# Laying the exponentials of a cross-attention block by quarters of the keys before their regrouping transfers

## The chip, the cores and the metric

The kernel runs on one core of one Trainium2 chip. The metric is the time on the device in microseconds, lower being better. The time before is a median of 3 runs.

## The reference

Two cross-attention layers follow each other, with 4 batches of 1024 queries (512 features) and 1024 context rows (384 features), all in float32. The change is in layer 0, which has 16 heads of 64:

```python
h = layernorm(x, gamma, beta)
Q, K, V = h @ Wq, context @ Wk, context @ Wv          # 16 heads of 64
attn = softmax(Q K^T, over the 1024 keys) * 64**-0.5
x = x + (attn V) @ Wo + bo
```

Layer 1 has 16 heads of 32, rotates and normalises its queries and keys, takes a softmax over the same 1024 context rows, and adds its output to x.

## The kernel before

**Tiling.** Batches follow each other. Within layer 0 of a batch the heads are taken in 8 pairs p, and within a pair the queries in 8 tiles i of 128. One step (p, i) is `Attention0.step`. Two steps of one pair make a block (`BQ = 2`), so a batch has 32 blocks and the kernel has 128.

**A step.** `scores` (L372) multiplies 128 queries by 1024 keys for both heads of the pair, into two PSUM tiles `s`. For each head VectorE takes the negative maximum of a row (L393), and ScalarE writes the exponentials to the tile `e` of the block and sums them in the same instruction (L394). VectorE then transposes `e` in place, in blocks of 32 x 32 (L399). This leaves the keys of a 32 x 32 block on the partitions, but only within each group of 32 partitions. At the end of a block, 16 transfers from SBUF to SBUF (L406) regroup the rest: transfer (g, q) takes the quarter g of the keys from the 32 partitions that held the queries of group q, and puts it on the 32 partitions of group g in the tile `eT`. VectorE inverts the sums (L410).

**Product.** `product` (L451) multiplies the values by `eT` for a whole block, as 16 matmuls in the program (8 groups of keys, 2 heads), each over 256 queries. A block is kept in `self.blocks` and its product is issued two blocks later in program order: in an even step, when two blocks are waiting. `factors` (L424) spreads the inverted sums on GpSimd, `factors_turned` (L442, L443) turns them over through TensorE and copies them to `vals` on ScalarE, and L458 multiplies them with the product.

**Buffers.** `e` and `eT` have two buffers each (tags `e` and `big`), which layer 1 also uses. The exponentials of a block so wait for the transfers of the block two before. `s` has two buffers, one for each head, so the scores of a step wait for the exponentials of the step before.

**Order.** The order on each engine is the program's. Other TensorE work (projections of later pairs at L158, output projections, layer 1's first projections) stands in a list of units, `work`, each with a cost in microseconds, and `fill` issues units between the parts of a step. All loads and stores, and the 16 transfers of a block, stand on SP's queue in program order. At the start of a pair, loads of weights (`pair_load`, L313; `wo_load`, L665), loads of x (L287) and, in the first pairs of later batches, stores of the batch before (L848) stand between two blocks' transfers. L188 and L279 load context rows and x rows. Layer 1 (L599 to L657) follows, with its own exponentials, sums (L615, L619), rotations (L501) and products (L638, L649).

Of the kernel before, what the change touches and what calls it, by code (L numbers as in the profile page):

```python
# [30 lines left out]
F32 = mybir.dt.float32  # L31
AF = mybir.ActivationFunctionType
# [3 lines left out]
P = 128  # L36
S = 1024
# [70 lines left out]
def xattn_kernel(ctx: ExitStack, tc: tile.TileContext, a: dict, out: bass.AP):  # L108
    nc = tc.nc
# [4 lines left out]
    sb = ctx.enter_context(tc.tile_pool(name="sb", bufs=2))  # L114
# [54 lines left out]
    def flush():  # L169
        while posts:  # L170
            posts.pop(0)()
# [185 lines left out]
    BQ = 2  # L357
    r = [slice(j * HD0, (j + 1) * HD0) for j in range(2)]

    class Attention0:  # L360
# [20 lines left out]
        def step(self, p, i, pr, us):  # L381
            n = f"{self.b}_{p}_{i}"
            sc = self.scores(p, i, pr)
            if i % BQ == 0 and len(self.blocks) == 2:
                self.factors_turned()
            m = sb.tile([P, 2], F32, tag="m", bufs=3, name=f"m_{n}")
            l = sb.tile([P, 2], F32, tag="l", bufs=3, name=f"l_{n}")
            if i % BQ == 0:
                self.e = sb.tile([P, BQ, 2, S], F32, tag="e", bufs=2, name=f"e0_{n}")
                self.li = sb.tile([P, BQ, 2], F32, tag="li", bufs=4, name=f"li_{n}")  # L390
            e = [self.e[:, i % BQ, j, :] for j in range(2)]
            for j in range(2):
                nc.vector.tensor_reduce(m[:, j : j + 1], sc[j], AX.X, ALU.max, negate=True)  # L393
                nc.scalar.activation(e[j], sc[j], AF.Exp, bias=m[:, j : j + 1], accum_out=l[:, j : j + 1])  # L394
            holds["posts"] = True
            self.u.fill(min(us, 1.8))
            holds["posts"] = False
            for j in range(2):
                nc.vector.transpose(e[j], e[j])  # L399
            flush()  # L400
            if i % BQ == BQ - 1:
                eT = sb.tile([P, 2 * BQ, 4, S // 4], F32, tag="big", bufs=2, name=f"eT_{n}")
                of = self.e.rearrange("p t h s -> p (t h) s")
                for g in range(4):
                    for q in range(4):
                        nc.sync.dma_start(  # L406
                            eT[32 * g : 32 * (g + 1), :, q, :],
                            of[32 * q : 32 * (q + 1), :, g * (S // 4) : (g + 1) * (S // 4)],
                        )
            nc.vector.reciprocal(self.li[:, i % BQ, :], l)  # L410
            if i % BQ == BQ - 1:
                eT = eT.rearrange("p (t h) a s -> p h t a s", h=2)
                self.blocks.append((p, i // BQ, pr, eT, self.li))
            elif self.blocks:
                if len(self.blocks) == 2:
                    self.product()
                self.factors()
            self.u.fill(us - min(us, 1.8))
# [322 lines left out]
    for b in range(B):  # L741
# [6 lines left out]
        for p in range(NPAIR):  # L748
# [15 lines left out]
            elif p % 2 == 0:  # L764
                i = p // 2 - 1
# [4 lines left out]
                    lambda n, i=i: wo[i][:, n % 2, :],  # L770
# [29 lines left out]
            for i in range(NT):  # L800
# [8 lines left out]
                n = NT * (NPAIR - p if later else 1) - i  # L809
# [15 lines left out]
        q = rotated_chains(qT, xnT, NQ, lambda k, wq=wq: wq[0][:, k, :], f"q1_{b}_0", tmp)  # L825
# [25 lines left out]
        for half in range(2):  # L851
            n = 0
# [94 lines left out]
```

## Time and profile before

| | |
|---|---|
| median of 3 runs | 2992.65 us (2991.08 to 2992.93) |
| profiled execution: time / span | 2989.95 us / 2987.7 us |
| mean granted TensorE clock | 0.996 |
| busy: TensorE / VectorE / ScalarE / GpSimd | 98% / 75% / 48% / 14% |
| packets on SP's queue | 371,664, with 343.43 MB |
| regrouping transfers L406 | 2048 of 128 KB |

A row of the costliest groups reads: line, engine, operation, output<-input by tile name, shape, count | busy us in total, mean ns of one | idle us of the engine just before them, and what ended most of it. A row of the timeline reads: start us, length us, engine, line, operation, tiles, count, and in brackets the idle time before it with what ended it; a "q" after the engine's name means its queue. A row of the windows reads: the stretch, its length, the busy time of each engine in it (TensorE, its weight loads, VectorE, ScalarE, GpSimd) with instruction counts, the granted share of the TensorE clock, the busy share of the DMA engines and GB/s.

### The profile page before, as it was taken

What the parts mean: (1) busy time and instruction counts of PE and PEld (TensorE: products, weight loads), DVE (VectorE), ACT (ScalarE), POOL (GpSimd) and SP (SyncE); (2) the same over time, 40 slices, a digit from 0 to 9 for tenths busy, and PEclk for the clock granted to TensorE, in tenths of its full rate; (3) what the DMA queues carried; (4) which work ended last, traced back from release to release, by engine and by line L of the source; (5) the groups of instructions that cost most, each with busy time, mean ns of one, the idle gap of its engine ahead of it and who ended that gap; (6) DMA issues with size and microseconds to landing.
All of it is one profiled execution on the core that took longest, in us unless ns stands there. A gap on an engine that the chain in (4) does not pass through costs nothing.

```text
span 2987.7 us, 60793 instructions
## 1 busy us (share of the span) xinstructions
PE 2917.3 (98%) x24748; PEld 1544.2 (52%) x24748; DVE 2230.7 (75%) x2824; ACT 1429.5 (48%) x2265; POOL 416.6 (14%) x392
## 2 busy tenths in 40 slices
PE   8999999999999999999999999999999999999998
PEld 5544546555544555655554454555455445455544
DVE  4777795877777779587777777958777777795777
ACT  3444443666443444465644344446664444444664
POOL 0010022420000002232000000223200000022310
PEclk9999999999999999999999999999999999999999
DMA  5788674010387867301048776730104978772000
GB/s 148 169 192 180 158 178 112 22 35 25 81 203 185 186 163 171 94 21 35 25 98 207 175 183 166 171 84 21 35 25 113 205 176 182 170 169 69 2 2 30
DMA packets 374134, 348.50 MB, mean 117 GB/s; under 512 B 37600, under 2 KB 355296, under 8 KB 373856
## 3 DMA queue, kind: packets, MB, share of 16 engines
q1 hardware_dynamic: 371664, 343.43, 48.4%
q8 instruction: 197, 3.23, 0.5%
q10 hardware_dynamic: 2192, 1.19, 0.2%
q14 instruction: 81, 0.66, 0.1%
HBM read 67.64 MB, written 8.39 MB: 25 GB/s over the span
## 4 chain that ended last, share of the span: by engine, by line
PE 78%; DVE 10%; DMA 4%; SPq 3%; ACT 2%; issue 1%; POOL 1%; DVEq 0%; ACTq 0%
PE s L372 14%; PE av L451 13%; PE po L158 10%; PE pv L158 7%; PE s L599 7%; PE av L638 6%; PE pqT L158 6%; PE pkT L158 5%; PE q_p L158 3%; DMA eT<-e 2%; SPq L406 2%; PE av L649 2%; DVE both L615 2%; DVE e L399 2%; PE k_p L158 1%; DVE m L393 1%
## 5 line engine op out<-in xcount | busy, mean ns | idle before, releaser
L394 ACT ACTIVATE e<-s,m 128x1024 f32<-128x1024 f32 x512 | 565.6, 1109 | 679.2 <-DVE m L393 613.8
L393 DVE TENSOR_REDUCE m<-s 128x1 f32<-128x1024 f32 x512 | 602.8, 1219 | 320.0 <-PE s L372 320.0
L399 DVE STREAM_TRANSPOSE e<-e 128x1024 f32<-128x1024 f32 x512 | 606.7, 1224 | 54.9 <-ACT e L394 43.0
L609 ACT ACTIVATE e<-s 128x1024 f32<-128x1024 f32 x512 | 496.5, 1022 | 315.1 <-PE s L599 300.1
L372 PE MATMUL s<-qk 64*128 64x512 f32 x2048 | 520.5, 615 | 6.0 <-ACT e L394 5.3
L451 PE MATMUL av<-eT,v 128*64 128x256 f32 x4096 | 474.8, 385 | 15.6 <-DMA eT<-e 13.7
L615 DVE TENSOR_TENSOR both<-e 128x512 f32<-128x512 f32 x512 | 342.4, 701 | 127.7 <-ACT e L609 92.5
L451 PEld LDWEIGHTS av<-eT,v 128*64 128x64 f32 x4096 | 289.4, 138 | 214.0 <-issue 53.7
L372 PEld LDWEIGHTS s<-qk 64*128 64x128 f32 x2048 | 181.8, 186 | 262.6 <-issue 188.9
L599 PE MATMUL s<-q,k 32*128 32x256 f32 x4096 | 305.7, 402 | 5.8 <-ACT q L526 2.7
L599 PEld LDWEIGHTS s<-q,k 32*128 32x128 f32 x4096 | 191.6, 185 | 149.7 <-ACT e L609 71.4
L158 PE MATMUL po<-wo,vals 128*128 128x512 f32 x512 | 239.6, 601 | 2.5 <-ACT v L130 2.5
L158 PE MATMUL pqT<-hT,w 128*128 128x512 f32 (+1 forms) x800 | 241.3, 597 | 0.7 <-ACT hT L255 0.7
L443 ACT COPY vals<-rT 128x256 f32<-128x256 f32 x128 | 47.7, 372 | 327.4 <-PE rT L442 327.4
L301 DVE TENSOR_TENSOR x<-x,po 128x512 f32<-128x512 f32 x200 | 133.8, 679 | 82.8 <-PE po L158 82.8
L158 PEld LDWEIGHTS pv<-w,cT 128*128 128x128 f32 (+1 forms) x2400 | 176.7, 152 | 30.3 <-issue 27.2
L158 PE MATMUL pv<-w,cT 128*128 128x128 f32 (+1 forms) x2400 | 186.5, 275 | 0.0
L158 PE MATMUL pkT<-cT,w 128*128 128x512 f32 (+1 forms) x600 | 181.6, 599 | 1.1 <-ACT cT L130 1.1
L619 DVE TENSOR_TENSOR both<-both 128x1024 f32<-128x1024 f32 x128 | 159.7, 1248 | 4.4
L158 PEld LDWEIGHTS po<-wo,vals 128*128 128x128 f32 x512 | 90.9, 190 | 106.4 <-issue 101.4
L158 PEld LDWEIGHTS pqT<-hT,w 128*128 128x128 f32 (+1 forms) x800 | 85.9, 151 | 112.2 <-issue 105.9
L638 PE MATMUL av<-e,v 128*32 128x256 f32 x2048 | 137.0, 385 | 0.0
(461 smaller groups left out, 2667.0 us busy)
## 6 DMA issues: line engine op xcount, KB each, us to landing
eT<-e SPq DMA_DIRECT2D x2048, 128.0 KB, 2.8
xr<-in_x_dram SPq DMA_DIRECT2D x32, 256.0 KB, 4.3
x<-in_x_dram SPq DMA_DIRECT2D x32, 256.0 KB, 3.8
wo<-in_Wo_dram SPq DMA_DIRECT2D x16, 512.0 KB, 4.2
out_dram<-x SPq DMA_DIRECT2D x32, 256.0 KB, 2.7
w<-in_Wq_dram SPq DMA_DIRECT2D x31, 256.0 KB, 4.0
c<-in_ctx_dram SPq DMA_DIRECT2D x32, 192.0 KB, 4.5
wkv<-in_wkv_dram SPq DMA_DIRECT2D x16, 384.0 KB, 3.5
```

The source lines that it names most:

```text
L158: nc.tensor.matmul(o[rr], lhsT[:, rr], rhs, start=start, stop=stop)
L301: nc.vector.tensor_add(xt[t], xt[t], pp[0])
L372: nc.tensor.matmul(sc[j][:, kb * 512 : (kb + 1) * 512], pr["qT"][r[j], i * P : (i + 1) * P], pr["kT"][r[j], kb * 512 : (kb + 1) * 512], st ...
L393: nc.vector.tensor_reduce(m[:, j : j + 1], sc[j], AX.X, ALU.max, negate=True)
L394: nc.scalar.activation(e[j], sc[j], AF.Exp, bias=m[:, j : j + 1], accum_out=l[:, j : j + 1])
L399: nc.vector.transpose(e[j], e[j])
L451: nc.tensor.matmul(av[r[j], :W].rearrange("p (t a i) -> p t a i", t=BQ, a=4), pr["v"][:, k, r[j]], eT[:, j, :, :, k * 32 : (k + 1) * 32], ...
L599: nc.tensor.matmul(sc[j // 2][:, j % 2, c, :], kT[rr, g, k * P : (k + 1) * P], qT[rr, g, qb * WQ : (qb + 1) * WQ], start=True, stop=True,)
L609: nc.scalar.activation(e, sc[u], AF.Exp, scale=float(np.sqrt(np.float32(HD1))))
L615: nc.vector.tensor_add(self.both[:, kk, 2 * u : 2 * u + 2, :], es[u][:, :, 0, :], es[u][:, :, 1, :])
L619: nc.vector.tensor_add(self.both[:, 0], self.both[:, 0], self.both[:, kk])
L638: nc.tensor.matmul(self.av[rr, 0, :], v[g][:, 2 * kk + c, rr], es[j // 2][:, j % 2, c, :], start=first and c == 0, stop=end and c == 1,)
```

## The change

The tile `e` was laid by step, head and key. It is now laid by quarter of the keys first, and then by step and head. The exponentials of one step and head are written as four pieces of 256, a quarter apart, and the transposes read and write the same four pieces. The tile `eT` is laid by group of queries first, and then by step and head. So a regrouping transfer moves, for each of its 32 partitions, one piece of 4 KB on both sides, where it moved four pieces of 1 KB. Bytes, the number of transfers, their order and the arithmetic are the same. The product reads the same elements of `eT` at other distances.

```diff
             if i % BQ == 0:
-                self.e = sb.tile([P, BQ, 2, S], F32, tag="e", bufs=2, name=f"e0_{n}")
+                self.e = sb.tile([P, 4, BQ * 2, S // 4], F32, tag="e", bufs=2, name=f"e0_{n}")
                 self.li = sb.tile([P, BQ, 2], F32, tag="li", bufs=4, name=f"li_{n}")
-            e = [self.e[:, i % BQ, j, :] for j in range(2)]
+            e = [self.e[:, :, i % BQ * 2 + j, :] for j in range(2)]
             for j in range(2):
                 nc.vector.tensor_reduce(m[:, j : j + 1], sc[j], AX.X, ALU.max, negate=True)
-                nc.scalar.activation(e[j], sc[j], AF.Exp, bias=m[:, j : j + 1], accum_out=l[:, j : j + 1])
+                nc.scalar.activation(e[j], sc[j].rearrange("p (g s) -> p g s", g=4), AF.Exp, bias=m[:, j : j + 1], accum_out=l[:, j : j + 1])
...
             if i % BQ == BQ - 1:
-                eT = sb.tile([P, 2 * BQ, 4, S // 4], F32, tag="big", bufs=2, name=f"eT_{n}")
-                of = self.e.rearrange("p t h s -> p (t h) s")
+                eT = sb.tile([P, 4, BQ * 2, S // 4], F32, tag="big", bufs=2, name=f"eT_{n}")
                 for g in range(4):
                     for q in range(4):
-                        nc.sync.dma_start(
-                            eT[32 * g : 32 * (g + 1), :, q, :],
-                            of[32 * q : 32 * (q + 1), :, g * (S // 4) : (g + 1) * (S // 4)],
-                        )
+                        nc.sync.dma_start(eT[32 * g : 32 * (g + 1), q], self.e[32 * q : 32 * (q + 1), g])
             nc.vector.reciprocal(self.li[:, i % BQ, :], l)
             if i % BQ == BQ - 1:
-                eT = eT.rearrange("p (t h) a s -> p h t a s", h=2)
+                eT = eT.rearrange("p a (t h) s -> p h t a s", h=2)
                 self.blocks.append((p, i // BQ, pr, eT, self.li))
```

## The prediction

> **What bounds the kernel now.** I read the busy table first, then the costliest groups, then the list of waits of TensorE, then the timeline at the longest of those waits.
>
> ```profile
> PE 2917.3 (98%) x24748; PEld 1544.2 (52%) x24748; DVE 2230.7 (75%) x2824; ACT 1429.5 (48%) x2265; POOL 416.6 (14%) x392
> ...
> L399 DVE STREAM_TRANSPOSE e<-e 128x1024 f32<-128x1024 f32 x512 | 606.7, 1224 | 54.9 <-ACT e L394 43.0
> ...
> L451 PE MATMUL av<-eT,v 128*64 128x256 f32 x4096 | 474.8, 385 | 15.6 <-DMA eT<-e 13.7
> ```
>
> TensorE is busy 98% of the span: 2987.7 - 2917.3 = 70.4 us is all that is open. What the change touches (exponentials, transposes, 2048 transfers) is on other engines, so it pays only where TensorE waits for it, or works slowly because it has waited. Those waits, longest first (us in total, times, longest):
>
> ```profile
> PE av L649 <- DVE both L615: 15.4, 9, 2.2
> PE av L451 <- DMA eT<-e: 13.7, 6, 3.3
> ...
> PE av L451 <- DMA x<-in_x_dram: 1.3, 1, 1.3
> ...
> PE av L451 <- DMA w<-in_Wv_dram: 0.3, 1, 0.3
> ```
>
> The first belongs to layer 1, which the change leaves alone. The other three are one thing: the av product of a block (L451) is reached before its regrouped tile eT has landed; in the last two the landings of eT and of a load are close together, and I count all 15.3 us to eT. The listing of L406 and the timeline show how long eT takes and what a late one does:
>
> ```profile
> L406 SPq DMA_DIRECT2D eT<-e x2048: 585/601/2250, 42.4 to 2708.0; - x187
> ...
> DMA to landing us min/median/max: 2.4/2.8/9.2
> ```
> ```profile
> 1639.75 12.86 SPq L406 DMA_DIRECT2D eT<-e  x16
> ...
> 1652.65 0.59 SPq L287 DMA_DIRECT2D x<-in_x_dram  x1
> ...
> 1657.09 1.11 ACT L394 ACTIVATE e<-s,m 128x1024 f32<-128x1024 f32 x1 [3.63 <-DMA eT<-e]
> 1657.18 6.45 PE L451 MATMUL av<-eT,v 128*64 128x256 f32 x32 [3.27 <-DMA eT<-e]
> ```
>
> SP needs 0.60 us to issue one of the 16 transfers of a block, 11.5 to 12.9 us for all, and the last lands about 3 us later. The av product then starts 3.27 us late and takes 6.45 us, where the same 32 instructions take 3.67 elsewhere in the timeline (at 408.09, for one). The next view has the reason in its TensorE clock column (after the last engine), and the rates of the DMA engines (last two columns: share, GB/s):
>
> ```profile
> 1630.00:1635.00 5.00, 5.00 (x19) 2.06 (x16) 3.33 (x6) 1.39 (x3) 0.00 (x0) 1.00 0.87 205
> 1637.00:1641.00 4.00, 4.00 (x18) 1.40 (x18) 1.71 (x4) 0.88 (x3) 0.40 (x1) 1.00 1.00 307
> 1644.00:1648.00 4.00, 4.00 (x16) 1.55 (x13) 2.54 (x5) 0.37 (x1) 0.00 (x0) 1.00 1.10 186
> 915.33:918.74 3.41, 3.41 (x20) 2.38 (x18) 2.32 (x3) 2.63 (x5) 0.00 (x0) 0.50 0.88 209
> 1656.02:1662.85 6.83, 5.67 (x28) 3.58 (x30) 2.42 (x3) 2.77 (x5) 0.00 (x0) 0.50 0.96 187
> ```
>
> After two of the late landings (915, 1656) the clock is granted at 0.50. That costs 6.45 - 3.67 = 2.78 us at 1657 and, with the av product at 915.05 taking 5.36, 1.69 us there: 4.5 us. Late landings so cost 15.3 + 4.5 = 19.8 us. The rates: eT alone, paced by SP, moves 205 GB/s (0.87 share); HBM loads and stores 307 GB/s; eT with a backlog only 186 GB/s at a share of 1.10. With a backlog it is the DMA engines that limit, not SP.
>
> [...] Every eT transfer reads 32 partitions and writes 32. [...] 186 to 205 GB/s, against 307 for transfers over 128 partitions. [...] the trace shows 0.50 in stretches of 3.41 and 6.83 us, but after waits of 2.13 and 3.27 us, and none after the 3.12 us wait at 2398.49.
>
> **The change part by part.**
>
> 1. *Exponentials* (L394, 512 of 1109 ns) write four pieces of 256, 4 KB apart. Nearest row: the copy qk<-pkT (L130), which writes its result scattered in pieces of 32, takes 585 ns and its plain twin qk<-pqT 583. Price 0 to +0.01 us, taken 0. ScalarE is 48% busy and covers it.
> 2. *Transposes* (L399, 512 of 1224 ns) now name 4x256 columns. The trace has no such form. Bounds: 0, or a start-up per piece. L615 (512 columns, 701 ns) and L619 (1024, 1248 ns) give 1.07 ns a column and 0.15 us of start-up, so three more would be 0.46 us each. No gain is excluded from the other side, but none has a reason. I take 0: L501, over a pattern in pieces, takes 677 to 691 ns against 679 for the plain L301.
> 3. *av products* (L451, 4096 of 385 ns) read the same eight runs of 32 columns at other distances. L638 reads one run of 256 and takes 385 too: price 0. It can't be hidden (TensorE), so any nanosecond would cost 4 us; hence it stays in the range.
> 4. *Waits in the instruction list.* By the program's order, TensorE loses 240 waits on its own earlier scores (two ahead of each odd step's scores) and 28 others; the other engines' order and the semaphores they wait for are as before. Price 0: scores follow the av product with those waits (425.25 after 421.65 + 3.67) as closely as they follow po without (404.94 after 403.99 + 1.02), overlapping by 0.07 us in both. SP's queue keeps its order: 16 transfers a block, each waiting for one eight places earlier.
> 5. *Transfers.* 2048 x 32 partitions x 4 pieces of 1 KB = 262,144 packets become 65,536 of 4 KB. Issue: the nearest plain pattern, c (L188) and xr (L279), takes 371 ns at the median, 327 at least; I take 371, at most 601 as now. Moving: [...] at the measured 186 GB/s 0.70 us. So SP stops being the limit[...]. I take 0.62 us (an estimate[...]): 16 x 0.62 = 9.9 us against 11.5 (SP at 1623.57: 11.48 us), **1.6 us earlier** a block.
> 6. *What stands behind eT on SP.* At 1635.10 SP comes to stores and loads (4.6 us of issue, about 2 MB) that precede the late block, whose transposes end at 1637.22; SP starts that block 2.5 us late, at 1639.75. With the block before done 1.6 us sooner, these too drain 1.6 us sooner. The late block gains both: 3.2 us.
>
> Sum. The waits (1.2 to 3.3 us each, the small ones less) fall by 3.2 us in the blocks behind loads; I leave 3 us standing in all, for landings that loads behind them disturb: 15.3 - 3 = 12.3. The half clock goes with its waits: 4.5, of which I count 3.2 since it did not follow every wait. Sum 15.5 us. Next in line at those places is the copy of vals (L443, done at 1653.46 there), which is before the product by 3.6 us, so nothing takes over at once. The 56.2 us that ScalarE waits for eT shrink as well, at no price or gain: they are beside TensorE's work.
>
> The profiled execution took 2989.95 us with a span of 2987.7; the median of the runs is 2992.65, 2.7 us more. I take the sum off the median: 2992.65 - 15.5 = **2977 us**.
>
> **Rivals.**
>
> *Nothing lands earlier* (0.16 for within 0.2%). The issue keeps its 0.585 us, because it is the SBUF-to-SBUF copy that is dear, not the pieces (both sides have four pieces now, so the trace can't separate these)[...]. For it: a share of 1.10 with little to gain from fewer packets. Against: eT paced by SP already moves 205. It gives 0 to -6 us: 2987 to 2993.
>
> *SP was the limit alone.* Then a block's issue is 16 x 0.371 = 5.9 us and eT lands 5 us sooner; all 19.8 us go, and up to 5 us of score waits (5.3 us for L394 in TensorE's list): 2968. [...]
>
> *Slower: the transposes pay for each piece.* 2 x 0.46 = 0.92 us a step on VectorE. Most steps have 320.0 / 256 = 1.25 us of VectorE waiting for scores (the total that L393 waits) and hide it. The steps that carry layer 1's rotations (pairs 6 and 7, 16 of 64 in each of 4 batches) have none: the scores at 430.87 already wait 1.32 us for L394. 64 x 0.92 = 59 us at most, half of it 29, less the 15.5 gained: 3006. It decides from about 0.25 us a transpose. Against: pieces are free in L501. The same side is reached if av loses 4 ns an instruction.
>
> **How the numbers follow.** A measurement of this kernel tells about 0.2%, 6 us, from no change. Forecast and its stronger form: 0.60 and 0.14, together 0.74 faster. Nothing lands earlier: 0.16. Slower: 0.10. Low end 2967 (SP alone the limit), high end 2992 (no gain); what is left out is the slower case and a little of the same.
>
> **What would show it.** Right: about 175,000 packets on SP's queue (371,664 - 196,608); L406 near 371 ns; "PE av L451 <- DMA eT" under 4 us; no 0.50 clock after an av wait; L394, L399 and L451 within 1% of 1109, 1224 and 385. Step 2 is wrong if L399 is over 1.3 us, step 5 if eT keeps 0.6 us of issue or its windows stay at 186 to 205 GB/s with the waits standing, step 3 if av's mean rises. The prediction is wrong if TensorE's waits for eT fall and the span doesn't.

## The result, and the profile after

Over six runs each, the changed kernel takes 2981.30 us (2979.04 to 2985.07) and the kernel before 2991.86 us (2988.97 to 2997.24): a ratio of 0.9962, with a 95% interval of 0.9951 to 0.9974. That is a gain of 10.6 us (7.8 to 14.7), where 15.5 us were forecast, and the time is 4.3 us over the 2977 of the forecast. The profiled execution takes 2979.04 us with a span of 2976.8 us, 10.9 us less than the one before.

The busy table and the three groups that the change touches, in the page of the kernel after (L396, L401 and L449 are the exponentials, transposes and product that were L394, L399 and L451):

```profile
PE 2914.2 (98%) x24748; PEld 1541.9 (52%) x24748; DVE 2228.5 (75%) x2824; ACT 1429.5 (48%) x2265; POOL 416.5 (14%) x392
...
L396 ACT ACTIVATE e<-s,m 128x1024 f32<-128x1024 f32 x512 | 565.6, 1109 | 666.7 <-DVE m L395 623.1
...
L401 DVE STREAM_TRANSPOSE e<-e 128x1024 f32<-128x1024 f32 x512 | 606.6, 1223 | 46.9 <-ACT e L396 41.1
...
L449 PE MATMUL av<-eT,v 128*64 128x256 f32 x4096 | 470.3, 382 | 7.8 <-DMA eT<-e 6.2
```

The four-piece patterns are free: 1109 and 1223 ns, as before, and the product does not get slower. In the profiled executions the gain has two parts. TensorE's idle time goes from 70.4 to 2976.8 - 2914.2 = 62.6 us, which is 7.8 us, and its busy time goes down by 3.1 us. The list of TensorE's waits says where the idle time went:

```profile
PE av L449 <- DMA eT<-e: 6.2, 5, 1.8
...
PE av L449 <- DMA w<-in_Wq_dram: 0.9, 1, 0.9
PE av L449 <- DMA x<-in_x_dram: 0.7, 1, 0.7
```

The product's waits for landings were 15.3 us and are 7.8. That is 7.5 of the 7.8 us. The listing of the transfers' line, and the timeline at the block that cost most before:

```profile
L407 SPq DMA_DIRECT2D eT<-e x2048: 507/590/2020, 43.3 to 2697.3; - x187
...
DMA to landing us min/median/max: 2.2/2.4/8.6
```
```profile
1633.28 12.33 SPq L407 DMA_DIRECT2D eT<-e  x16
...
1649.71 3.67 PE L449 MATMUL av<-eT,v 128*64 128x256 f32 x32 [0.89 <-DMA eT<-e]
```

The issue of a transfer fell only from 601 to 590 ns, and a transfer lands 2.4 us after its issue, not 2.8. In the block shown the product waits 0.89 us, not 3.27, and then takes the usual 3.67 us, not 6.45: the clock is granted at 1.00 from 1649 to 1655, and in the kernel before it was 0.50 at this product. No stretch at half clock follows a product in this execution. The two of before (4.5 us) are gone, but one has come after a wait of 2.22 us in layer 1, and none followed the same wait before:

```profile
2102.24:2105.65 3.41, 3.41 (x30) 1.36 (x28) 2.85 (x3) 0.58 (x1) 3.33 (x2) 0.50 0.02 5
```

It costs up to half of 3.41 us. 4.5 - 1.7 = 2.8 us is nearly all of the 3.1 us of busy time. How much falls to the waits and how much to the clock changes from one execution to the next, as e7 shows below.

SP's queue has 175,056 packets (371,664 before), so each partition's 4 KB really is one packet.

### The profile page after: what moved, and what is told of

Its sections match the earlier page's. It is cut to its first block, busy times and chain, and to the rows that moved or that the text cites. A ratio compares the mean times of both kernels' runs of the same rounds, so it can differ in the third digit from the quotient of the medians.

```text
span 2976.8 us, 60525 instructions
## 1 busy us (share of the span) xinstructions
PE 2914.2 (98%) x24748; PEld 1541.9 (52%) x24748; DVE 2228.5 (75%) x2824; ACT 1429.5 (48%) x2265; POOL 416.5 (14%) x392
## 3 DMA queue, kind: packets, MB, share of 16 engines
q1 hardware_dynamic: 175056, 343.43, 48.8%
## 4 chain that ended last, share of the span: by engine, by line
PE 82%; DVE 8%; DMA 3%; SPq 3%; ACT 2%; issue 1%; POOL 1%; ACTq 0%; DVEq 0%
PE s L372 15%; PE av L449 13%; PE po L158 10%; PE s L597 7%; PE pv L158 7%; PE av L636 6%; PE pqT L158 6%; PE pkT L158 5%; PE q_p L158 3%; PE av L647 2%; SPq L407 2%; PE k_p L158 2%; DVE both L613 2%; DMA eT<-e 1%; PE rT L440 1%
## 5 line engine op out<-in xcount | busy, mean ns | idle before, releaser
L396 ACT ACTIVATE e<-s,m 128x1024 f32<-128x1024 f32 x512 | 565.6, 1109 | 666.7 <-DVE m L395 623.1
L401 DVE STREAM_TRANSPOSE e<-e 128x1024 f32<-128x1024 f32 x512 | 606.6, 1223 | 46.9 <-ACT e L396 41.1
L449 PE MATMUL av<-eT,v 128*64 128x256 f32 x4096 | 470.3, 382 | 7.8 <-DMA eT<-e 6.2
L449 PEld LDWEIGHTS av<-eT,v 128*64 128x64 f32 x4096 | 285.5, 137 | 205.3 <-issue 50.2
```

Of the source, the lines that this page charges most:

```text
L396: nc.scalar.activation(e[j], sc[j].rearrange("p (g s) -> p g s", g=4), AF.Exp, bias=m[:, j : j + 1], accum_out=l[:, j : j + 1])
L449: nc.tensor.matmul(av[r[j], :W].rearrange("p (t a i) -> p t a i", t=BQ, a=4), pr["v"][:, k, r[j]], eT[:, j, :, :, k * 32 : (k + 1) * 32], ...
```

## The experiments

All ratios are to runs of the kernel before on the same chip. "Late blocks" are the six blocks that stand behind loads and stores, the first of pairs 1 and 2 in the last three batches. Their time from the first issue to the last landing is read from the trace: 16.7 us on average before and 16.2 after (15.9 in e7, the same kernel again). Over all blocks the median of the same time is 13.1 us before and 12.6 after. A table behind e9 splits the time of the late blocks.

### e1 and e2: one side of the layout alone

e1 keeps the tile e as it was, so a transfer reads four pieces and writes one:

```diff
-                self.e = sb.tile([P, 4, BQ * 2, S // 4], ...)
+                self.e = sb.tile([P, BQ, 2, S], ...)
...
+                of = self.e.rearrange("p t h (g s) -> p g (t h) s", g=4)
-                        nc.sync.dma_start(eT[32 * g : 32 * (g + 1), q], self.e[32 * q : 32 * (q + 1), g])
+                        nc.sync.dma_start(eT[32 * g : 32 * (g + 1), q], of[32 * q : 32 * (q + 1), g])
```

> The tile e is laid as before (the transfer reads four pieces of 1 KB), eT as after (it writes one of 4 KB). Theory A (only a piece that is whole on both sides counts; the gain is earlier landings): packets stay at 1 KB (371,664 on SP's queue), issue 585 to 601 ns, landing 2.8 us, TensorE waits 12 to 16 us for eT, time within 0.15% of before (2990 +-4). Theory B (the issue price follows the number of access dimensions): issue between 507 and 590 ns and a part of the gain. This kernel keeps TensorE's 240 waits on its own scores, so theory C (their removal is the gain) expects the time of before too, and the next kernel tells it apart.

e2 keeps eT as it was, so a transfer reads one piece and writes four:

```diff
-                eT = sb.tile([P, 4, BQ * 2, S // 4], ...)
+                eT = sb.tile([P, 2 * BQ, 4, S // 4], ...)
...
-                        nc.sync.dma_start(eT[32 * g : 32 * (g + 1), q], self.e[32 * q : 32 * (q + 1), g])
+                        nc.sync.dma_start(eT[32 * g : 32 * (g + 1), :, q, :], self.e[32 * q : 32 * (q + 1), g])
```

> The tile e is laid as after (exponentials and transposes in four pieces, TensorE without the 240 waits on its own scores), eT as before (one piece read, four written). Theory A (earlier landings): 1 KB packets, landing 2.8 us, waits for eT of 12 to 16 us, time within 0.15% of before (2990 +-4). Theory C (the 240 waits): the gain of after, 2981 +-3. If the four-piece patterns of ScalarE and VectorE cost or gain anything, it shows here against before: 0 expected.

Measured: e1 1.0004 (0.9994 to 1.0014), e2 0.9993 (0.9983 to 1.0003). In both, the issue takes 585/601 ns (minimum/median), the landing 2.8 us, and SP's queue has 371,664 packets. The waits, of e1 and then of e2:

```profile
PE av L450 <- DMA eT<-e: 13.6, 7, 3.9
```
```profile
PE av L449 <- DMA eT<-e: 11.2, 6, 2.8
```

So theory A holds: of the four layouts only the one with a piece that is whole on both sides has larger packets (175,056 on SP's queue) and lands sooner (2.4 us). (e2's waits are a little under the 12 to 16 us expected.) e2 has the exponentials and transposes in four pieces, and TensorE without its 240 waits for itself, and comes out like before within 0.2%. This prices these parts together at nothing; the exponentials and transposes are also free one by one, by their own times (1109 and 1223 ns in e2). Theory C is out, and so is B.

### e3: what sets the 590 ns

Each transfer is split into two of half the bytes. Theory P is that the 590 ns go with the bytes moved, theory F that they go with the transfer.

```diff
-                        nc.sync.dma_start(eT[32 * g : 32 * (g + 1), q], self.e[32 * q : 32 * (q + 1), g])
+                        for t in range(2):
+                            tt = slice(2 * t, 2 * t + 2)
+                            nc.sync.dma_start(eT[32 * g : 32 * (g + 1), q, tt], self.e[32 * q : 32 * (q + 1), g, tt])
```

> As after, but each transfer is split into two of 64 KB (pieces of 2 KB, 32 transfers a block, 4096 in all). Theory P [...]: a transfer of 64 KB is issued in about 300 to 350 ns, a block takes about as long as in after, time 2978 to 2990. Theory F (a transfer has a fixed issue price): each still takes 507 to 590 ns, a block 32 x 0.6 = 19 us, more than the some 14 us that two steps take, SP becomes the limit in layer 0, and the time goes up by some 128 x 5 us = 600 us, to about 3600.

Measured: 3978 us, a ratio of 1.3309 (1.3291 to 1.3327). The listing of its transfers and TensorE's longest wait:

```profile
L409 SPq DMA_DIRECT2D eT<-e x4096: 507/588/1897, 32.2 to 3695.2; - x196
```
```profile
PE av L451 <- DMA eT<-e: 750.5, 126, 12.6
```

Theory F: 64 KB take as long to issue as 128 KB, 588 and 590 ns at the median. It is a price per transfer, not per byte. The 600 us that I expected were too little; TensorE alone waits 750.5 us, and its mean clock is 0.890, where it was 0.997 in the kernel after.

### e4: neighbours in the queue on other halves of the partitions

In the kernel after, the four transfers of a group g follow each other, so that four write to the same 32 partitions, and eight to the same half. e4 puts the same 16 transfers in an order where each next one writes to the other half and, but for one step of the 15, reads from the other half. Theory P is that late landings come of the old order, theory F that they come of the issue:

```diff
-                for g in range(4):
-                    for q in range(4):
-                        nc.sync.dma_start(eT[32 * g : 32 * (g + 1), q], self.e[32 * q : 32 * (q + 1), g])
+                for d in (0, 2):
+                    for g in range(2):
+                        for q in range(2):
+                            for h in (0, 2):
+                                g2, q2 = g + h, q + (h + d) % 4
+                                nc.sync.dma_start(eT[32 * g2 : 32 * (g2 + 1), q2], self.e[32 * q2 : 32 * (q2 + 1), g2])
```

> As after, with the 16 transfers of a block in another order: each following one reads from the other half of the partitions (0 to 63, 64 to 127) and writes to the other half than the one before. Theory P [...]: [...] packets of 4 KB take near 200 ns rather than 299, the rate with a backlog rises over 250 GB/s, the waits for eT fall from 7.8 us (with those put down to loads) to under 3, time 2973 to 2978. Theory F (issue is the limit): rate and landing in the steady state stay (205 GB/s), blocks behind loads gain a little or nothing, time 2978 to 2983.

Measured: 2969.33 us, 0.9937 (0.9925 to 0.9949). No wait of the product for eT is left in TensorE's list. The listing and SP's row at the late block of pair 2 in the third batch, and the product there, which has no wait in brackets:

```profile
L410 SPq DMA_DIRECT2D eT<-e x2048: 507/590/2128, 43.2 to 2687.1; - x187
```
```profile
1628.62 11.93 SPq L410 DMA_DIRECT2D eT<-e  x16
```
```profile
1644.00 3.67 PE L452 MATMUL av<-eT,v 128*64 128x256 f32 x32
```

The issue is as dear as in after, and the late blocks take 13.1 us rather than 16.2. So with a backlog the time follows the order of the transfers, at the same 590 ns of issue. Windows of 4 us in the late block, where eT is transferred with a backlog, of after and then of e4 (last column GB/s; 186 in such a window before):

```profile
1637.00:1641.00 4.00, 4.00 (x30) 1.91 (x26) 2.74 (x4) 1.07 (x2) 0.00 (x0) 1.00 1.09 220
```
```profile
1632.30:1636.30 4.00, 4.00 (x30) 1.86 (x26) 2.69 (x4) 1.02 (x2) 0.00 (x0) 1.00 1.07 246
```

The block shown has the highest rate of the six in after. The same stretch, from 4 to 8 us behind the first issue, has 180 GB/s before, 185 in after, 195 in e7 and 218 in e4 as the mean of the six late blocks. So the order raised the rate, and the layout hardly did.

Parts of the expectation failed: a packet of 4 KB took 294 ns at the median (299 in after), not 200, the rate stayed under 250 GB/s, and the time came out under the 2973 to 2978 us expected. What keeps a packet at 294 ns is not shown.

### e5: the order alone

The alternating order of e4 in the kernel before, with its pieces of 1 KB. If late landings come of the old order alone (theory P), the waits go.

```diff
...
+                                nc.sync.dma_start(
+                                    eT[32 * g2 : 32 * (g2 + 1), :, q2, :],
+                                    of[32 * q2 : 32 * (q2 + 1), :, g2 * (S // 4) : (g2 + 1) * (S // 4)],
+                                )
```

> The kernel before, with its four pieces of 1 KB, but with the 16 transfers of a block in the alternating order of e4. [...] the order alone takes the waits for eT from 15 us to under 3 and the time to 2969 to 2974, and the layout adds little on top. If the small pieces are what the backlog pays for (theory S), the waits stay over 8 us and the time is 2978 to 2990.

Measured: 2968.60 us, 0.9930 (0.9915 to 0.9946), with no product waiting for eT. Late blocks take 14.4 us. That is enough to be in time, so the further 1.3 us of e4 (13.1), which has the layout too, bring nothing: e4 and e5 do not differ beyond their intervals.

### e6 and e7: the loads in front

e6 takes the load of Wo out of the queue in front of the first block of pairs 2, 4 and 6 and issues it behind that block; e7 is the changed kernel again.

```diff
-                wo[i] = wo_load(a["Wo"], i, f"wo0_{b}_{i}")
...
+                if i == 2 and p > 1 and p % 2 == 0:
+                    wo[p // 2 - 1] = wo_load(a["Wo"], p // 2 - 1, f"wo0_{b}_{p // 2 - 1}")
```

> As after, but the load of Wo (512 KB, in the pairs 2, 4 and 6) is issued two steps later, behind the first block's transfers. If the backlog in front of a pair's first block makes its landing late, the waits of the pairs 2 (0.9 to 1.8 us each in after, 4.0 us in three batches) go and those of the pairs 1 (0.7 to 1.6 us, 3.0 us) stay: TensorE waits some 3 to 4 us for eT, time 2976 to 2979. If the landing is late by SP's own delay and the transfers' rate alone, little changes: 2980 to 2983.

> The changed kernel again, for a comparison with e5 and e6 on one chip: 0.995 to 0.998 of before, TensorE waits of 6 to 9 us for eT (with those put down to loads).

Measured: e6 2975.06 us, 0.9950 (0.9935 to 0.9966); e7 2979.00 us, 0.9969 (0.9957 to 0.9980). e7's waits for eT, 4.6 us and 0.4 us more that the list puts down to issue, were under the range expected, and under the 7.8 us of the first profile of the same kernel. In e6, 2.8 us are left for eT. In two of the three batches the wait of pair 2 is gone; in the second batch (913.25) 1.29 us stand, and the waits of the pairs 1 stand (0.69, 0.57, 0.22). The waits of the pairs 2 sum to 1.3 us in e6, where they are 4.0 in after and 3.8 in e7. So the backlog in front counts, as expected, though the difference in time to e7 lies within the intervals.

e7 also shows that a part of a time is the clock's. Against the execution before, TensorE waits 59.5 us in all and not 70.4, but is busy for 2922.0 us and not 2917.3: this profiled execution has half-clock stretches that belong to no late landing, as the second and third of these (the first follows a product that waited 1.89 us):

```profile
914.56:917.97 3.41, 3.41 (x18) 2.39 (x16) 2.25 (x2) 2.70 (x5) 0.00 (x0) 0.50 1.04 199
429.86:436.69 6.83, 6.83 (x26) 2.97 (x24) 5.35 (x6) 2.67 (x5) 0.81 (x2) 0.50 0.60 138
1170.56:1177.39 6.83, 6.83 (x22) 2.84 (x24) 4.88 (x6) 2.86 (x6) 1.22 (x3) 0.50 0.70 184
```

### e8 and e9: reading or writing

e8 alternates the half that is read, e9 the half that is written:

```diff
 e8
                 for g in range(4):
-                    for q in range(4):
+                    for q in (0, 2, 1, 3):
 e9
-                for g in range(4):
-                    for q in range(4):
+                for q in range(4):
+                    for g in (0, 2, 1, 3):
```

> As after, but within a group g the queries' groups q go 0, 2, 1, 3: neighbours in the queue read from alternating halves of the partitions, and still write to the same quarter four times in a row. If the write side is what backs up (theory W), little changes against after: blocks behind loads take 15.4 to 16.6 us from first issue to last landing, waits for eT of 4 to 8 us, 2977 to 2983. If the read side is (theory R), it does what e4 did: 13 us, no waits, 2966 to 2972. If each is a limit of its own, neither e8 nor e9 reaches e4.

> As after, but q is the outer loop and within it g goes 0, 2, 1, 3: neighbours in the queue write to alternating halves and read from the same quarter four times in a row. Theory W: it does what e4 did, 13 us for a block behind loads, no waits, 2966 to 2972. Theory R: like after, 15.4 to 16.6 us, 2977 to 2983.

Measured: e8 2978.68 us, 0.9955 (0.9942 to 0.9968); e9 2969.28 us, 0.9925 (0.9912 to 0.9939). TensorE's list has this row in e8 and none of its kind in e9:

```profile
PE av L449 <- DMA eT<-e: 4.7, 5, 1.4
```

e8 has one more wait of 0.4 us, put down to a load of x. Late blocks take 15.5 us in e8 and 13.9 us in e9. Theory W holds: what shortens a late block is alternating the half written (13.9 us), and hardly the half read (15.5, where after has 16.2). e9 reads four times from the same 32 partitions and is as fast as e4.

The mean times of the six late blocks in each run's one profile, in us, split at the landing of the first of their 16 transfers:

| | first issue to last landing | to the first landing | from the first to the last landing |
|---|---|---|---|
| before | 16.7 | 7.4 | 9.3 |
| after (e7) | 16.2 (15.9) | 6.7 (6.4) | 9.5 (9.5) |
| e4, both halves alternate | 13.1 | 5.8 | 7.2 |
| e5, the same order in before | 14.4 | 7.2 | 7.3 |
| e8, the half read alternates | 15.5 | 6.4 | 9.1 |
| e9, the half written alternates | 13.9 | 6.4 | 7.5 |

The two parts answer to different things. The last column follows the order of the writes: in a row, the transfers land 0.62 (before) and 0.63 us (after) apart, about as far as SP issues them (0.60 and 0.59), so a backlog hardly drains; alternated, the first eight land 0.40 to 0.43 us apart. The column before it, which holds what stood in front, is what the layout shortens: 7.1 to 7.4 us in the four kernels with packets of 1 KB (before, e1, e2, e5), 5.8 to 6.7 in those with 4 KB and 128 KB a transfer.

One rival is left. Neighbours in e9 differ in the half and in the group of 32 partitions that they write to, and no run alternates the groups within one half. That it is the half and not the 32 partitions is not shown by these runs.

## Why the prediction was right, and where its sizes were off

**What bounds the kernel.** Right. The gain is where the product waited for eT and where the clock fell after it: 7.5 us of waits and the two stretches of 4.5 us, less a new one elsewhere. The waits are shorter in both profiles of the changed kernel (7.8 and 5.0 us) than in the three of kernels with packets of 1 KB and the old order (15.3 before, 13.9 in e1, 11.4 in e2).

**Steps 1 to 4** (patterns, product, TensorE's waits for itself). Right: 1109, 1223 and 382 ns, e2 at 0.9993 with all of these edits but the product's, and e1 at 1.0004 with the product's.

**Step 5, the issue price.** Wrong, by the sign that I had given for it: eT kept its 0.6 us. I took 371 ns from the loads of c and xr. Measured are 507 ns for a transfer that is not close behind another and 590 ns in a row. The rival "nothing lands earlier" had named the reason, that a copy within SBUF is dear to issue and not its pieces. e3 shows that bytes don't matter and e1, e2 that pieces on one side alone don't. What makes it dearer than a load is not separated here: it differs both in the source and in having 32 partitions. The trace before held a warning that I passed over. The loads of x have the same shape as those of xr, but mostly stand right behind a copy:

```profile
L287 SPq DMA_DIRECT2D x<-in_x_dram x32: 433/590/803, 106.0 to 2420.3; - x32
```

The 25 of them right behind a copy take 590 ns at the median, while the loads of xr take 328 alone and 431 behind each other. So a load behind a copy is about as dear as the copy (601), and 371 was no price for a row. "SP stops being the limit" is therefore wrong for a block without backlog. Its time fell only by 0.4 us (13.1 to 12.6), not by 1.6; most of it is the landing of the last transfers.

**Step 5, the rate.** The size was right, the gain was not there. I took 0.62 us for moving a transfer. That was my estimate and no trace showed it: the 205 and 186 GB/s of the trace before make 0.64 and 0.70 us for 131,072 B. In the late blocks the transfers landed 0.63 us apart after the change, but 0.62 us apart before it, so larger packets brought no rate where there was a backlog. That is 207 and 211 GB/s; the 186 that I went by was one window of 4 us. Nor did the share of the DMA engines tell the limit: in the windows shown it is 1.10, 1.09 and 1.07 at 186 (before), 220 (after) and 246 GB/s (e4). What I did not look at is where neighbours in the queue write. The order of the loops in g and q sends eight writes in a row to one half of the partitions, and with larger packets that is as before. In e4, e5 and e9 an order that alternates the written half takes away every wait of the product for eT (15.3 us before, 7.8 after), with either size of packet.

**Step 6, what stands behind eT.** The mechanism is shown by e6, which moves a load; the size was not there, since the blocks before were not done 1.6 us sooner. Both gains together were to be 3.2 us in a late block. They were 1.1: on average SP starts the six late blocks 1.6 us after their last transpose and not 2.3, and their own time is 0.5 us shorter, all of it ahead of the first landing. In the block shown the wait fell by 2.4 us, elsewhere by less (2.13 to 1.76 at the second batch's pair 2). This is the term that was mis-sized: 3 us of waits were to stand, 7.8 stood (5.0 in e7), so 7.5 us were gained (10.3) and not 12.3.

**The half clock.** Forecast 3.2 us, measured 3.1 us of busy time, but e7 shows such a stretch after a late product again, and several elsewhere, and is busy 4.7 us longer than before. This agreement is luck.

**The total.** That 10.6 us came of 15.5 is in part luck as well. That eT lands sooner where TensorE waits for it was right. But it was to land 3.2 us sooner by a cheaper issue, and landed 1.1 us sooner with an issue about as dear as before.

**The rivals.** "Nothing lands earlier" had the issue right, but eT did land sooner (2.4 us after its issue, not 2.8). "SP was the limit alone" is out by the issue price. "Slower by pieces in the transposes" is out by 1223 ns. The sum was 12.3 + 3.2 = 15.5; it came out as 7.5 + 3.1 + 0.3 (other waits) = 10.9 in the profiled executions, and 10.6 in the medians (e7: 0.9969 of before, which is 9 us).

**Better than both.** e4, e5 and e9 at about 2969 us, 0.7% under before. For this kernel, the order of the transfers is worth twice the layout, at two changed lines in e9, and with it the layout adds nothing that these runs can tell.

## What to carry to other kernels

When a transfer is late, ask whether its issue, its packets or its place in a queue makes it so, and look at a stretch where the queue is full and at one where it is not: here packets four times as large gave 0.4 us of 13 in the one and 0.5 of 16.7 in the other. Before the pieces are reshaped, look at which partitions neighbours in the queue write to; alternating the halves took the late blocks from 16.2 to 13.1 us (e4) at no cost. A wait of TensorE may cost more than its length: here the clock was granted at 0.50 after two waits of 2.13 and 3.27 us, and the two products behind them took 4.5 us longer. So small waits are worth a look even at 98% busy.

## What the runs showed of the hardware that was not expected

- Issuing a copy within SBUF over 32 partitions from SP takes 507 ns alone and 590 ns in a row, whether it moves 64 or 128 KB (588 and 590 ns at the median); with four pieces on either side or both, 585 and 601 ns. Loads of 128 partitions with one piece each (c, xr) take 328 ns alone and 431 right behind one another, but 590 right behind a copy (x in the kernel before, where the copy takes 601).
- Copies in a row that write to one quarter of the partitions, and to one half, land further apart behind loads than copies whose writes alternate; which partitions are read hardly matters. In a late block 16 copies land, from the first to the last, within 9.1 to 9.5 us in the first case and within 7.2 to 7.5 us when the writes alternate (e8 and after against e9, e4 and e5). Whether the quarter or the half counts is open.
- Half-clock stretches of TensorE come and go between executions of one kernel: in the changed kernel none followed a product's wait for eT in one profiled execution, and one did in another, where there were four others besides before the last 12 us.
